# A macaron block (FFN, dilated attention, FFN) on one core: token mix taken from the PSUM tile, mask folded into the bias, square moved to ScalarE, projection operands split into 16-bit halves

## The chip, the cores and the metric

The kernel runs on one core of a Trainium2 chip. The core has a matrix engine (TensorE, PE in the profile; its weight loads have a row of their own, PEld), a vector engine (VectorE, DVE), a scalar engine (ScalarE, ACT), a general engine (GpSimd, POOL) and a queue engine (SyncE, SP) that issues most of the transfers. The engines run side by side, each takes its instructions in a fixed order, and they wait for one another through semaphores. Matrix products are written to PSUM, everything else lives in SBUF; the transfers go between SBUF and the device's memory.

The metric is the device time of one execution in microseconds (us). The time before is given as the median of three runs, and one further execution was recorded with the profiler.

## The reference, cut to what matters

There are 8 sequences of 1024 tokens with 256 channels, and 16 heads of 16 channels. Three residual steps follow one another: half an FFN, the attention, and half the same FFN.

```python
x = x + 0.5 * ffn(layernorm(x));  x = x + attn(layernorm(x));  x = x + 0.5 * ffn(layernorm(x))

def ffn(x):
    x_prev = shift x by one token (zero at the start of a sequence)
    xr = mu_r * x + (1 - mu_r) * x_prev
    xk = mu_k * x + (1 - mu_k) * x_prev
    return sigmoid(xr @ W_r) * (square(relu(xk @ W_k)) @ W_v)

def attn(x):
    q, k, v = split(x @ qkv_w.T + qkv_b)
    for i, o in enumerate(OFFSETS):            # 0..32, 48, 64, 96, 128, 192, 256, 384
        lg = (q . shift(k, o)) * inv * (1 + q . scale_embed[i]) + pos_bias[i]
        lg = where(pos >= o, lg, -1e30)
    p = softmax over the offsets
    out = (sum over i of p[i] * shift(v, o)) * if_gain
    return (out * sigmoid(x @ gate_w.T + gate_b)) @ out_w.T + out_b
```

## The kernel before, in words

The work is cut into 32 chunks of 256 tokens (two blocks of 128) and, for the attention proper, into 64 blocks of 128 tokens. Five stages are written as Python generators:

- `stage_f1`, the first FFN, one chunk a step, loads the chunk and leaves it in `x1`;
- `stage_p`, the projections of a chunk to q, k, gate and v, which sends q and k (as 16-bit high and low halves, tile `hl`) and v to device memory in layouts from which later stages read them back;
- `stage_qk`, the score products of half a sequence, copied out of PSUM by L308 and written to device memory, from which they are read back skewed, so that one offset is one column;
- `stage_att`, one block: the logits in tile `lg` (128 x 40 offsets x 16 heads), the softmax, the far offsets as products on POOL (L445) added up on DVE (L457), the near ones as matrix products (L464 transposes, then `pv`), the gate and the output projection;
- `stage_f2`, the second FFN, which also stores the result.

The order of the work is set in three ways. The last lines (L515 to L522) sort the steps of the five stages by hand-set offsets, `TRACE` for the order in which they are traced and `RANK` for their priority. The tile framework then fixes every engine's order of instructions at build time, from these priorities and a simulated timeline. On the chip each engine follows that order and stops at the first instruction whose inputs or buffers are not there. Every PSUM tag has one buffer: an FFN lane (`a` or `b`) has a single bank for its transposed input `tr` and then, one after the other, for the three products `p`, so each of them needs the one before to have been read.

One FFN chunk (`ffn`, L165 to L215) goes like this. `norm_stats` makes mean and 1/sd (DVE, and six small POOL instructions). `norm_transposed` applies them on ACT (L160) and transposes the chunk on PE (L162) into the PSUM tile `tr`, channels on partitions. ACT copies `tr` to the SBUF tile `xt` (L186), which is one column wider: POOL puts the last column of the previous chunk in front (L185, or L183 sets it to zero at the start of a sequence) and keeps the last column for the next one (L189). DVE takes the difference of the two shifted views (L193, 512 elements a partition) and then, twice for `xk` and twice for `xr`, adds mu times the difference to the shifted view (L196, 256 elements each). PE multiplies `xk` by W_k (the K product), ACT applies relu (L201), POOL squares in place (L207). PE multiplies `xr` by W_r (the R product), ACT applies tanh (L206), PE multiplies the square by W_v (the V product), DVE combines (L212), and POOL adds the result to the chunk (L213). Tiles `xt`, `xk` and `xr` have one buffer for each lane. There are 64 such chunks in the two stages.

In `stage_p` (L233 to L295) the transposed chunk is split into `xh` (F32R, copied on ACT, L244) and the rest `xl` (L245, DVE); `wa_hi` and `wa_lo` are the same split of the weights, made in `load_att`. Each of the four projections is 12 matrix products of 256 columns: high by high, high by low and low by high (L134 is the helper that issues every product). In `stage_att`, POOL adds the position bias to the logits (L419) and, for the first three of the eight blocks of a sequence, the mask (L421).

Of the kernel before, what the change touches and what calls it, by code (L numbers as in the profile page):

```python
# [8 lines left out]
F32 = mybir.dt.float32  # L9
F32R = mybir.dt.float32r  # L10
F16 = mybir.dt.float16
I32 = mybir.dt.int32
AF = mybir.ActivationFunctionType
ALU = mybir.AluOpType
# [25 lines left out]
F2A = 28  # L40
TRACE = (0, 3.6, -4.4, -8.1, -10.6)
# [8 lines left out]
def macaron(ctx: ExitStack, tc: tile.TileContext, x, wffn, watt, wo, cols, rows, pbias, se, mask, out):  # L50
# [14 lines left out]
    bias = const.tile([128, NO * 16], F32, name="bias")  # L65
    msk = const.tile([128, 3, NO], F32, name="msk")
    wa_hi = const.tile([128, 4, 2, 256], F32R, name="wa_hi")
    wa_lo = const.tile([128, 4, 2, 256], F32R, name="wa_lo")
    seb = const.tile([128, 2, NO], F16, name="seb")
    half = const.tile([128, 4], F32, name="half")  # L70
# [18 lines left out]
    def load_ffn():  # L89
        nc.sync.dma_start(w_f, wffn.rearrange("w (c p) d -> p w c d", p=128))  # L90
        nc.vector.tensor_scalar(w_f[:, 2], w_f[:, 2], 0.25, None, ALU.mult)

    def load_att():
        with tc.tile_pool(name="setup", bufs=1) as sp:
            wst = sp.tile([128, 4, 2, 256], F32, name="wst")
            nc.sync.dma_start(wst, watt.rearrange("w (c p) d -> p w c d", p=128))
            nc.vector.tensor_scalar(wst[:, 0], wst[:, 0], 0.25, None, ALU.mult)
            nc.vector.tensor_copy(wa_hi, wst)
            nc.vector.tensor_tensor(wa_lo, wst, wa_hi.bitcast(F32), ALU.subtract)
            nc.vector.tensor_scalar(b_q, b_q, 0.25, None, ALU.mult)  # L100
            nc.vector.tensor_scalar(b_g, b_g, 0.5, None, ALU.mult)
            nc.sync.dma_start(row, rows.unsqueeze(0).to_broadcast([128, 2, 256]))
            for t in [t.bitcast(F32) for t in kb] + vw:
                nc.gpsimd.memset(t, 0.0)
# [8 lines left out]
            nc.sync.dma_start(bias, pbias.to_broadcast([128, NO * 16]))  # L113
            nc.sync.dma_start(msk, mask.rearrange("t p u -> p t u"))
            nc.sync.dma_start(wot, wo.rearrange("(c p) d -> p c d", p=128))
            for c in range(2):
                nc.vector.tensor_scalar(wot[:, c], wot[:, c], gain[:, c : c + 1], 0.5, ALU.mult, ALU.mult)
# [47 lines left out]
    def ffn(take, done, lane, singles):  # L165
# [3 lines left out]
        for c in range(NCH):  # L169
# [11 lines left out]
            xt = pw.tile([128, 2, 257], F32, name="xt", tag="xt" + s)  # L181
            if c % 4 == 0:
                nc.gpsimd.memset(xt[:, :, 0:1], 0.0)  # L183
            else:
                nc.gpsimd.tensor_copy(xt[:, :, 0:1], last)  # L185
            nc.scalar.copy(xt[:, :, 1:257], tr)  # L186
            if c % 4 < 3:
                last = pstat.tile([128, 2, 1], F32, name="last", tag="last" + s)
                nc.gpsimd.tensor_copy(last, xt[:, :, 256:257])  # L189
            xk = pw.tile([128, 2, 256], F32, name="xk", tag="xk" + s)  # L190
            xr = pw.tile([128, 2, 256], F32, name="xr", tag="xr" + s)
            prev = xt[:, :, 0:256]
            nc.vector.tensor_tensor(xr, xt[:, :, 1:257], prev, ALU.subtract)  # L193
            for o, mu in ((xk, mu_k), (xr, mu_r)):
                for h in range(2):
                    nc.vector.scalar_tensor_tensor(o[:, h], xr[:, h], mu[:, h : h + 1], prev[:, h], ALU.mult, ALU.add)  # L196
# [10 lines left out]
            nc.gpsimd.tensor_tensor(xk, xk, xk, ALU.mult)  # L207
# [25 lines left out]
    def stage_p():  # L233
        for c in range(NCH):
# [7 lines left out]
            xh = pw.tile([128, 2, 256], F32R, name="xh", tag="xk" + s)  # L242
            xl = pw.tile([128, 2, 256], F32R, name="xl", tag="xr" + s)
            nc.scalar.copy(xh, tr)  # L244
            nc.vector.tensor_tensor(xl, tr, xh.bitcast(F32), ALU.subtract)  # L245
# [26 lines left out]
            for g in range(2):  # L272
                nc.scalar.activation(gt[:, g], p[:, g], AF.Tanh, bias=b_g[:, g : g + 1], scale=0.5)
# [312 lines left out]
```

## Time and profile before

| | |
|---|---|
| Median of 3 runs | 1262.62 us (1255.21 to 1265.52) |
| The profiled execution | 1256.76 us |
| Its span, from the first to the last instruction | 1254.0 us |
| Mean granted TensorE clock | 0.956 |
| Device-memory traffic over the span | 224 GB/s |
| Share of the span that the core's DMA engines were busy, slices of 50 us from 150 to 1150 us | 0.71 to 0.92 |
| PE busy in 50 us, over the same slices | 41.1 to 48.1 us |
| DVE busy in 50 us, over the same slices | 28.9 to 45.3 us |

The profile gives each engine's busy time and share, groups of instructions (line, engine, operation, output <- input, partitions x elements) with count, busy time and mean duration, the waits between engines, and the chain of work that ended last, followed back from the last instruction. A busy share of PE is not PE at its peak, since matrix products overlap and their ends are modelled. Between the profiled execution's time and its span lie 2.76 us.

### The profile page before, as it was taken

What the parts mean: (1) busy time and instruction counts of PE and PEld (TensorE: products, weight loads), DVE (VectorE), ACT (ScalarE), POOL (GpSimd) and SP (SyncE); (2) the same over time, 40 slices, a digit from 0 to 9 for tenths busy, and PEclk for the clock granted to TensorE, in tenths of its full rate; (3) what the DMA queues carried; (4) which work ended last, traced back from release to release, by engine and by line L of the source; (5) the groups of instructions that cost most, each with busy time, mean ns of one, the idle gap of its engine ahead of it and who ended that gap; (6) DMA issues with size and microseconds to landing.
All of it is one profiled execution on the core that took longest, in us unless ns stands there. A gap on an engine that the chain in (4) does not pass through costs nothing.

```text
span 1254.0 us, 34712 instructions
## 1 busy us (share of the span) xinstructions
PE 1089.2 (87%) x13568; PEld 885.7 (71%) x13568; DVE 942.6 (75%) x2266; ACT 538.0 (43%) x1025; POOL 766.5 (61%) x1101
## 2 busy tenths in 40 slices
PE   2887989899799898989899989899988998888785
PEld 2676768677687677777777778786777787665664
DVE  7546768987587888879678866978858887877772
ACT  2444445344453444536345454544534444524231
POOL 7436619675575656659457564867656755657672
PEclk9999999899999999899999999999989999998988
DMA  8187888786878779787788977797787868998630
GB/s 263 32 224 222 241 242 265 229 238 194 251 226 254 230 233 274 221 252 232 193 260 257 254 201 230 228 269 227 233 243 234 269 197 254 284 280 265 202 99 24
DMA packets 256500, 282.88 MB, mean 226 GB/s; under 512 B 23440, under 2 KB 214608, under 8 KB 256336
## 3 DMA queue, kind: packets, MB, share of 16 engines
q1 hardware_dynamic: 247120, 263.36, 71.7%
q10 hardware_dynamic: 9216, 17.31, 3.8%
q8 instruction: 106, 1.74, 0.6%
q14 instruction: 58, 0.48, 0.1%
HBM read 151.67 MB, written 128.91 MB: 224 GB/s over the span
## 4 chain that ended last, share of the span: by engine, by line
PE 42%; DMA 25%; DVE 14%; SPq 6%; POOL 5%; issue 5%; ACT 4%; POOLq 0%; ACTq 0%; DVEq 0%
PE p L134 29%; DMA pd<-pd 9%; PE tra L464 4%; PE pv L134 3%; PE tra L134 3%; POOL prod L445 2%; DMA lg<-sl 2%; DMA x<-in_x_dram 2%; DMA qk<-hl 2%; DMA kb<-qk 2%; DMA sl<-sl 2%; DVE prod L457 2%; DVE xk L196 1%; PE gp L134 1%; DVE mx L423 1%
## 5 line engine op out<-in xcount | busy, mean ns | idle before, releaser
L134 PEld LDWEIGHTS <-qst 128*32 128x32 f16 (+1 forms) x5120 | 157.2, 120 | 100.1 <-issue 63.5
L134 PE MATMUL p<-kb,qst 128*32 128x128 f16 (+1 forms) x4096 | 185.1, 297 | 12.7 <-ACT sl L308 8.6
L308 ACT COPY sl<-p 128x512 f32<-128x512 f32 x224 | 130.8, 584 | 144.2 <-PE p L134 123.0
L445 POOL TENSOR_TENSOR prod<-v,lg 128x256 f32<-128x256 f32 x248 | 165.5, 687 | 10.2 <-ACT lg L425 6.1
L134 PE MATMUL p<-xk,w_f 128*128 128x256 f32 x512 | 144.9, 421 | 20.0 <-DVE xk L196 11.7
L419 POOL TENSOR_TENSOR lg<-lg,bias 128x640 f32<-128x640 f32 x64 | 113.5, 1774 | 71.8 <-DVE lg L410 66.9
L213 POOL TENSOR_TENSOR x<-x,xr 128x512 f32<-128x512 f32 x64 | 88.4, 1382 | 109.0 <-DVE xr L212 94.9
L457 DVE TENSOR_TENSOR prod<-prod 128x512 f32<-128x512 f32 (+2 forms) x120 | 126.1, 1051 | 32.1 <-POOL prod L445 31.5
L464 PE MATMUL tra<-ident,pd 128*128 128x128 f32 x512 | 97.1, 313 | 58.3 <-DMA pd<-pd 54.9
L160 ACT ACTIVATE xn<-x,nb,y 128x256 f32<-128x256 f32 x192 | 110.8, 602 | 63.0 <-DVE nb L152 55.2
L134 PE MATMUL p<-w_f,xk 128*128 128x256 f32 x512 | 132.9, 400 | 1.7 <-ACT xr L206 1.3
L134 PE MATMUL p<-w_f,xr 128*128 128x256 f32 x512 | 130.4, 396 | 3.6 <-ACT xk L201 2.8
L445 POOL TENSOR_TENSOR prod<-vn,lg 128x256 f32<-128x256 f32 x144 | 96.0, 678 | 54.3 <-ACT lg L425 35.4
L134 PE MATMUL p<-xh,wa_hi 128*128 128x256 f32 x384 | 123.2, 321 | 5.6 <-DVE hl L264 4.4
L134 PEld LDWEIGHTS p<-xk,w_f 128*128 128x128 f32 x512 | 99.3, 208 | 39.8 <-issue 10.5
L470 ACT COPY ptt<-tra 128x512 f32<-128x512 f32 x128 | 74.9, 585 | 116.1 <-PE tra L464 113.0
L464 PEld LDWEIGHTS tra<-ident,pd 128*128 128x128 f32 x512 | 71.0, 197 | 73.9 <-DMA pd<-pd 68.0
L263 ACT ACTIVATE hl<-p,col 128x256 f16<-128x256 f32 x128 | 60.6, 474 | 121.1 <-PE p L134 68.6
L134 PE MATMUL p<-xh,wa_lo 128*128 128x256 f32 x384 | 111.5, 290 | 0.0
L134 PE MATMUL p<-xl,wa_hi 128*128 128x256 f32 x384 | 111.4, 290 | 0.0
L134 PEld LDWEIGHTS p<-w_f,xr 128*128 128x128 f32 x512 | 95.3, 196 | 19.4 <-ACT xk L201 5.8
L134 PEld LDWEIGHTS p<-w_f,xk 128*128 128x128 f32 x512 | 96.0, 198 | 15.9 <-issue 2.8
(82 smaller groups left out, 2394.2 us busy)
## 6 DMA issues: line engine op xcount, KB each, us to landing
qk<-hl SPq DMA_DIRECT2D x256, 128.0 KB, 3.4
sl<-sl SPq DMA_DIRECT2D x256, 128.0 KB, 3.8
pd<-pd SPq DMA_DIRECT2D x64, 512.0 KB, 4.8
sf<-sl SPq DMA_DIRECT2D x184, 128.0 KB, 3.1
vw<-vd SPq DMA_DIRECT2D x128, 136.0 KB, 4.1
v<-vd SPq DMA_DIRECT2D x64, 272.0 KB, 4.3
lg<-sl SPq DMA_DIRECT2D x64, 264.0 KB, 4.1
pd<-lg ACTq DMA_DIRECT2D x64, 264.0 KB, 3.8
```

What stands on the lines that cost most here:

```text
L134: nc.tensor.matmul(o, l, r, start=start, stop=stop)
L160: nc.scalar.activation(xn, x2[:, i], AF.Identity, bias=nb[:, k : k + 1], scale=y[:, k : k + 1])
L196: nc.vector.scalar_tensor_tensor(o[:, h], xr[:, h], mu[:, h : h + 1], prev[:, h], ALU.mult, ALU.add)
L213: nc.gpsimd.tensor_tensor(x2, x2, xr, ALU.add)
L263: nc.scalar.activation(hl[:, 0], p[:, g], AF.Identity, bias=bb[:, g : g + 1])
L308: nc.scalar.copy(o[:, :, :, g], p.rearrange("n (q h j) -> n j h q", q=4, h=2))
L419: nc.gpsimd.tensor_tensor(la, la, bias, ALU.add)
L423: nc.vector.tensor_reduce(mx, lg.rearrange("p u e -> p e u"), AX.X, ALU.max)
L445: nc.gpsimd.tensor_tensor(prod[:, k], shifted[k][1]()[:, :, 0:16], lf[:, k].unsqueeze(2).to_broadcast([128, 16, 16]), ALU.mult,)
L457: nc.vector.tensor_tensor(o, terms[:, 0:m], terms[:, n - m : n], ALU.add)
L464: nc.tensor.transpose(tr[:, pr * 128 : pr * 128 + 128], pd.rearrange("p (m e) -> p m e", e=8)[:, :, 4 * g + pr], ident,)
L470: nc.scalar.copy(ptt.rearrange("p q n -> p (q n)"), tr)
```

## The change

It has four parts.

**Token mix.** The copy to `xt` and the difference go. For each of `xk` and `xr` and each half of the channels, ACT reads the PSUM tile and scales it by mu (the main term), and DVE adds (1 - mu) times the PSUM tile, shifted by one column, for columns 1 to 255. Column 0 gets its share of the previous chunk by one small POOL addition of `last`, which DVE has made from the last PSUM column (a product by `rest` = 1 - mu for all four). Both results are in one tile `xm`, with one buffer for each lane.

**Mask.** The bias tile becomes four: three with the mask of the first three blocks already added (three POOL additions in the setup), and one without.

**Square.** It moves from POOL (L207) to ACT.

**Projection.** `xh`, `xl`, `wa_hi` and `wa_lo` become F16 instead of F32R. The weights are multiplied by `WS` = 16 before the split, and the factor is taken out again where q.k is copied out of PSUM, in the gate's scale, in the logits' constant and in the output weights. The 12 products of a projection stay 12. `xh` and `xl` get buffers of their own.

```diff
+WS = 16.0
-    bias = const.tile([128, NO * 16], F32, name="bias")
-    msk = const.tile([128, 3, NO], F32, name="msk")
-    wa_hi = const.tile([128, 4, 2, 256], F32R, name="wa_hi")
-    wa_lo = const.tile([128, 4, 2, 256], F32R, name="wa_lo")
+    bias = const.tile([128, 4, NO, 16], F32, name="bias")
+    wa_hi = const.tile([128, 4, 2, 256], F16, name="wa_hi")
+    wa_lo = const.tile([128, 4, 2, 256], F16, name="wa_lo")
+    rest = const.tile([128, 4], F32, name="rest")
...
+        nc.vector.tensor_scalar(rest, col[:, 0:4], -1.0, 1.0, ALU.mult, ALU.add)
...
-            nc.vector.tensor_scalar(wst[:, 0], wst[:, 0], 0.25, None, ALU.mult)
-            nc.vector.tensor_copy(wa_hi, wst)
-            nc.vector.tensor_tensor(wa_lo, wst, wa_hi.bitcast(F32), ALU.subtract)
-            nc.vector.tensor_scalar(b_q, b_q, 0.25, None, ALU.mult)
+            nc.vector.tensor_scalar(wst[:, 0], wst[:, 0], 0.25 * WS, None, ALU.mult)
+            nc.vector.tensor_scalar(wst[:, 1:4], wst[:, 1:4], WS, None, ALU.mult)
+            nc.scalar.copy(wa_hi, wst)
+            nc.vector.tensor_tensor(wa_lo, wst, wa_hi, ALU.subtract)
+            nc.vector.tensor_scalar(b_q, b_q, 0.25 * WS, None, ALU.mult)
+            nc.vector.tensor_scalar(b_k, b_k, WS, None, ALU.mult)
...
+            nc.vector.tensor_scalar(bv, bv, WS, None, ALU.mult)
...
+            msk = sp.tile([128, 3, NO], F32, name="msk")
+            nc.sync.dma_start(bias[:, 3].rearrange("p u e -> p (u e)"), pbias.to_broadcast([128, NO * 16]))
             nc.sync.dma_start(msk, mask.rearrange("t p u -> p t u"))
+            for t in range(3):
+                nc.gpsimd.tensor_tensor(
+                    bias[:, t], bias[:, 3], msk[:, t].unsqueeze(2).to_broadcast([128, NO, 16]), ALU.add
+                )
...
-            xt = pw.tile([128, 2, 257], F32, name="xt", tag="xt" + s)
-            if c % 4 == 0:
-                nc.gpsimd.memset(xt[:, :, 0:1], 0.0)
-            else:
-                nc.gpsimd.tensor_copy(xt[:, :, 0:1], last)
-            nc.scalar.copy(xt[:, :, 1:257], tr)
+            xm = pw.tile([128, 2, 2, 256], F32, name="xm", tag="xm" + s)
+            for o, mu in ((1, mu_k), (0, mu_r)):
+                for h in range(2):
+                    x_, m = xm[:, o, h], rest[:, 2 * o + h : 2 * o + h + 1]
+                    nc.scalar.activation(x_, tr[:, h], AF.Identity, scale=mu[:, h : h + 1])
+                    nc.vector.scalar_tensor_tensor(x_[:, 1:256], tr[:, h, 0:255], m, x_[:, 1:256], ALU.mult, ALU.add)
+            if c % 4:
+                nc.gpsimd.tensor_tensor(xm[:, :, :, 0:1], xm[:, :, :, 0:1], last, ALU.add)
             if c % 4 < 3:
-                last = pstat.tile([128, 2, 1], F32, name="last", tag="last" + s)
-                nc.gpsimd.tensor_copy(last, xt[:, :, 256:257])
-            xk = pw.tile([128, 2, 256], F32, name="xk", tag="xk" + s)
-            xr = pw.tile([128, 2, 256], F32, name="xr", tag="xr" + s)
-            prev = xt[:, :, 0:256]
-            nc.vector.tensor_tensor(xr, xt[:, :, 1:257], prev, ALU.subtract)
-            for o, mu in ((xk, mu_k), (xr, mu_r)):
-                for h in range(2):
-                    nc.vector.scalar_tensor_tensor(o[:, h], xr[:, h], mu[:, h : h + 1], prev[:, h], ALU.mult, ALU.add)
+                last = pstat.tile([128, 2, 2, 1], F32, name="last", tag="last" + s)
+                nc.vector.tensor_tensor(
+                    last,
+                    tr[:, :, 255:256].unsqueeze(1).to_broadcast([128, 2, 2, 1]),
+                    rest.rearrange("p (o h u) -> p o h u", o=2, u=1),
+                    ALU.mult,
+                )
+            xk, xr = xm[:, 1], xm[:, 0]
...
-            nc.gpsimd.tensor_tensor(xk, xk, xk, ALU.mult)
+            nc.scalar.activation(xk, xk, AF.Square)
...
-            xh = pw.tile([128, 2, 256], F32R, name="xh", tag="xk" + s)
-            xl = pw.tile([128, 2, 256], F32R, name="xl", tag="xr" + s)
+            xh = pw.tile([128, 2, 256], F16, name="xh", tag="xh" + s)
+            xl = pw.tile([128, 2, 256], F16, name="xl", tag="xl" + s)
             nc.scalar.copy(xh, tr)
-            nc.vector.tensor_tensor(xl, tr, xh.bitcast(F32), ALU.subtract)
+            nc.vector.tensor_tensor(xl, tr, xh, ALU.subtract)
...
-            nc.scalar.copy(o[:, :, :, g], p.rearrange("n (q h j) -> n j h q", q=4, h=2))
+            nc.scalar.mul(o[:, :, :, g], p.rearrange("n (q h j) -> n j h q", q=4, h=2), WS**-3)
...
-            nc.gpsimd.tensor_tensor(la, la, bias, ALU.add)
-            if t < 3:
-                nc.gpsimd.tensor_tensor(lg, lg, msk[:, t].unsqueeze(2).to_broadcast([128, NO, 16]), ALU.add)
+            nc.gpsimd.tensor_tensor(la, la, bias[:, min(t, 3)].rearrange("p u e -> p (u e)"), ALU.add)
```

More of the change, by code (lines that the diff above doesn't have):

```diff
@@ L9 @@
 F32 = mybir.dt.float32
-F32R = mybir.dt.float32r
 F16 = mybir.dt.float16
@@ L112, in load_att @@
             nc.sync.dma_start(flat(pd_d, NL * 16, (4 * SKEW, 128), (SKEW, 4), (1, SKEW - NL * 16)), zero[:, : 4 * 512])
-            nc.sync.dma_start(bias, pbias.to_broadcast([128, NO * 16]))
+            msk = sp.tile([128, 3, NO], F32, name="msk")
+            nc.sync.dma_start(bias[:, 3].rearrange("p u e -> p (u e)"), pbias.to_broadcast([128, NO * 16]))
             nc.sync.dma_start(msk, mask.rearrange("t p u -> p t u"))
+            for t in range(3):
+                nc.gpsimd.tensor_tensor(
+                    bias[:, t], bias[:, 3], msk[:, t].unsqueeze(2).to_broadcast([128, NO, 16]), ALU.add
+                )
             nc.sync.dma_start(wot, wo.rearrange("(c p) d -> p c d", p=128))
             for c in range(2):
-                nc.vector.tensor_scalar(wot[:, c], wot[:, c], gain[:, c : c + 1], 0.5, ALU.mult, ALU.mult)
+                nc.vector.tensor_scalar(wot[:, c], wot[:, c], gain[:, c : c + 1], 0.5 / WS, ALU.mult, ALU.mult)
             se_f = sp.tile([128, NO], F32, name="se_f")
@@ L272, in stage_p @@
             for g in range(2):
-                nc.scalar.activation(gt[:, g], p[:, g], AF.Tanh, bias=b_g[:, g : g + 1], scale=0.5)
+                nc.scalar.activation(gt[:, g], p[:, g], AF.Tanh, bias=b_g[:, g : g + 1], scale=0.5 / WS)
             p = ps.tile([128, 512], F32, name="p", tag="ps" + s)
@@ L405, in stage_att @@
                 nc.vector.scalar_tensor_tensor(
-                    lg[:, 0:NL, e], gp[:, 0:NL], 1.0, lg[:, 0:NL, e], ALU.add, ALU.mult
+                    lg[:, 0:NL, e], gp[:, 0:NL], WS, lg[:, 0:NL, e], ALU.add, ALU.mult
                 )
@@ L412, in stage_att @@
                         gp[:, NL + k0 : NL + k1],
-                        1.0,
+                        WS,
                         ef[:, w0 : w1 + 1 : (w1 - w0) // (k1 - k0 - 1), e],
```

## The prediction

> **What bounds the kernel now.** I read the page first: the busy shares, then the chain that ended last.
>
> ```profile
> PE 1089.2 (87%) x13568; PEld 885.7 (71%) x13568; DVE 942.6 (75%) x2266; ACT 538.0 (43%) x1025; POOL 766.5 (61%) x1101
> ...
> PE 42%; DMA 25%; DVE 14%; SPq 6%; POOL 5%; issue 5%; ACT 4%; POOLq 0%; ACTq 0%; DVEq 0%
> PE p L134 29%; DMA pd<-pd 9%; PE tra L464 4%; PE pv L134 3%; PE tra L134 3%; POOL prod L445 2%; DMA lg<-sl 2%; DMA x<-in_x_dram 2%; DMA qk<-hl 2%; DMA kb<-qk 2%; DMA sl<-sl 2%; DVE prod L457 2%; DVE xk L196 1%; PE gp L134 1%; DVE mx L423 1%
> ```
>
> No engine is full all the time, and the end is passed from one to another: PE holds 42% of the chain, transfers 25%, DVE 14%. A microsecond taken from an engine is worth only the share of it that lies on the chain. I got those shares by going through the chain in windows of 20 us and adding its pieces by line: DVE 182.5 us in all, of it 10.3 on L193, 21.2 on L196 for `xk` and 15.0 for `xr`; POOL 63.4 (4.6 on the square, L207); ACT 46.9 (4.9 on the copy to `xt`, L186).
>
> Second, the groups by line and shape, for the price of what goes and of what is like what comes (last column: idle time before):
>
> ```profile
> L196 DVE SCALAR_TENSOR_TENSOR xk<-xr,col,xt 128x256 f32<-128x256 f32 x128 | 83.2, 689 | 0.5
> L196 DVE SCALAR_TENSOR_TENSOR xr<-xr,col,xt 128x256 f32<-128x256 f32 x128 | 82.3, 668 | 0.0
> ...
> L207 POOL TENSOR_TENSOR xk<-xk 128x512 f32<-128x512 f32 x64 | 74.0, 1156 | 53.1 <-ACT xk L201 52.6
> ...
> L193 DVE TENSOR_TENSOR xr<-xt 128x512 f32<-128x512 f32 x64 | 51.8, 810 | 10.8 <-ACT xt L186 10.7
> ...
> L425 ACT ACTIVATE lg<-lg 128x640 f32<-128x640 f32 x64 | 47.4, 741 | 58.9 <-DVE lg L424 25.5 <-POOL t L148 9.8 <-issue 8.8
> ...
> L186 ACT COPY xt<-tr 128x512 f32<-128x512 f32 x64 | 37.5, 586 | 6.5 <-PE tr L162 5.5 <-POOL t L149 0.9
> ...
> L421 POOL TENSOR_TENSOR lg<-lg,msk 128x640 f32<-128x640 f32 x24 | 31.7, 1323 | 0.6
> ...
> L273 ACT ACTIVATE gt<-p,col 128x256 f32<-128x256 f32 x64 | 26.8, 470 | 42.9 <-PE p L134 42.8
> ...
> L491 DVE SCALAR_TENSOR_TENSOR yt<-gt,tra 128x256 f32<-128x256 f32 x64 | 26.3, 410 | 24.7 <-PE tra L490 24.7
> ```
>
> A group's mean hides its spread, so third the tile views (shortest/median/longest ns):
>
> ```profile
> L196 DVE SCALAR_TENSOR_TENSOR xk<-xr,col,xt x128: 441/478/1785, 20.6 to 1239.1; 128x256 f32<-128x256 f32 x128
> ...
> L212 DVE SCALAR_TENSOR_TENSOR xr<-xr,p x64: 652/679/690, 35.4 to 1248.9; 128x512 f32<-128x512 f32 x64
> ```
>
> L196 reads two SBUF tiles and is stretched up to four times, while L212, which reads one operand from PSUM, never is. In the order of time the long ones lie beside running POOL instructions.
>
> **The token mix on DVE.** It goes from 51.8 + 83.2 + 82.3 = 217.3 us to 4 x 64 = 256 instructions of 255 elements, one operand in PSUM, one in SBUF. The nearest row is L491 (same operation, 256 elements, PSUM and SBUF): 410 ns, so 105.0 us. `last` is a tiny DVE read of PSUM like L481 (164 ns), 48 of them: 7.9 us. Sum 112.9, saved 104.4 us. Here the Trainium skill speaks against the change: its page "VectorE: DVE Perf Modes" (the section on the TRN2 errata) gives fixed costs of 58 cycles from SBUF and 120 from PSUM at 0.96 GHz, and its "Rules for kernel authors" advise copying PSUM to SBUF first where many operations follow. An estimate from that page: (58 + 256)/0.96 = 327 ns from SBUF against (120 + 255)/0.96 = 391 ns from PSUM, so the four additions cost 256 x 64 ns = 16 us more, only the difference (L193; by the page (58 + 512)/0.96 = 594 ns, 38 us) is saved, and with `last` 14 us remain of the 104. The row has 685 on the mean for SBUF and 410 for PSUM. I take the row, since the stretching is what this kernel pays. On the chain: L193 and L196 hold 46.5 us; at the same share of their work the new ones hold 46.5 x 112.9/217.3 = 24.2, so **-22.3 us** (by the page -46.5 x 14/217.3 = -3).
>
> **The token mix on ACT.** Four scalings of 256 elements from PSUM replace a copy of 512: L273 is such an instruction (PSUM, 256, one per-partition operand), 470 ns. 256 x 470 = 120.3 us for 37.5, +82.8 us. The square on ACT has no row of its own shape (512 elements from SBUF): L425 (640 elements from SBUF) bounds it from above at 741, L201 (512 from PSUM, 595) from below; I take 640, 41.0 us. Here the skill's page "ScalarE: Activation LUTs" (Rules for kernel authors) objects: products belong on VectorE. By the nearest row for that (L193, two SBUF operands, 512) the square would cost DVE 810 ns x 64 = 52 us of an engine that is 75% busy; ACT is 43% busy, so I follow the profile. At DVE's share on the chain (182.5/942.6 = 19%) the page's way would add 10 us, at ACT's (46.9/538.0 = 8.7%) 3.6. ACT rises to 538.0 + 82.8 + 41.0 = 662 us, 53%. On the chain: 8.7% x 123.8 = **+10.8 us**.
>
> **POOL** loses the square (74.0), the masks (31.7) and the column copies (L183 1.6, L185 14.3, L189 20.9): 142.5. It gets 48 small additions like L149 (290 ns), 13.9: net -128.6 us. At POOL's share on the chain (63.4/766.5 = 8.3%): **-10.6 us**. The square in itself is hidden: the V product needs its PSUM bank back from the tanh (L206), which comes after the R product; PE waited for the square 0.3 us in all. Without that cover, ACT's 640 ns still replace POOL's 1156 and a mean 1.4 us in POOL's queue.
>
> **Projection in 16 bits.** The order of time on PE shows what an F32R product takes from start to start:
>
> ```profile
> 678.06 0.29 PE L134 MATMUL p<-xl,wa_hi 128*128 128x256 f32 x1
> ...
> 678.18 0.28 PE L134 MATMUL p<-xh,wa_lo 128*128 128x256 f32 x1
> ...
> 678.30 0.28 PE L134 MATMUL p<-xh,wa_hi 128*128 128x256 f32 x1
> ```
>
> 0.12 us for 256 columns, while plain f32 products of the same size (8 in 1.89 us, less a tail of 0.38) step by 0.216. F32R is already the fast kind; the 16-bit form can't win a second factor of two. Bounds: nothing (other lanes' work fills the steps) to 12 ns a product (the F32R step is 118; half of the f32 step is 108). 1536 x 11 ns = 17 us of PE, x 42% = **-7 us**. Weight loads shrink from 196 to about 105 ns (the f16 row of that size), which overlap anyway.
>
> **With one answer.** L308's scaling instead of copying, the constants and the bias index: nothing, same instruction, same shape. The setup grows by three POOL additions (1323 each, 4.0 us), a 2048-element ACT copy and short DVE scalings, while the chain there runs through transfers and the SP queue until 26 us, and the first projection starts at 53 us; bounds 0 to +5, I take 0. No transfer is added or moved past a queue; the bias and mask loads stay where they are on SP.
>
> **What waits anew.** First, ACT's first scaling needs `xm`, which the last addition of the previous chunk (L213, POOL) still reads; behind it on ACT stand the copies of `sl`, `ptt` and `hl`. In the trace, the copy to `xt` began before the latest L213 had ended in 9 of 64 chunks, by 5.8 us in all: hidden. Second, the K product gets behind a POOL addition (column 0) and, since it needs the bank of `tr`, behind all four scalings and additions, `xr` too. POOL was late at L213 by a mean 1.04 us (up to 5.3), so the hop costs 1.04 + 0.29 us in 48 of 64 chunks, 1.0 us on the mean. Today (means over the 64 chunks, from the order of time) `xk` is complete 5.32 us after the copy to `xt` starts, `xr` 7.64 us, for 0.59 + 217.3/64 = 3.98 us of work: stretched 1.92 times by what else is in DVE's queue. The new work in line is 4 ACT steps (470, then 370 each, as the L273 pair ends after 840), one addition and `last`: 2.15 us, times 1.92 = 4.1, with the hop 5.1 us. The K product is late by -0.2 us: 0.
>
> **Sum:** -22.3 + 10.8 - 10.6 - 7 = -29.1 us: 1256.76 becomes 1227.7 for the profiled execution. The median of the runs shown lies 5.9 us above that execution, so for the median 1262.6 - 29.1 = **1234 us** (1233.5).
>
> **The rivals.** A: *the added latency doesn't shrink.* If the mix still takes 7.64 us from the copy to its end (ACT and DVE waiting for each other eight times a chunk) and POOL's hop comes on top, the K product starts 7.64 + 1.0 - 5.32 = 3.3 us later, and PE, in order, holds the products of other lanes behind it; behind those wait the copies of `sl` and `ptt` and the SP transfers. For this speaks that PE already waits for `xk`:
>
> ```profile
> PE p L134 <- DVE xk L196: 11.7, 13, 2.4
> ...
> PEld p L134 <- DVE xk L196: 9.2, 14, 1.9
> ```
>
> (total, times, longest), against it that it is only 13 of 64 chunks. The saving is eaten from 29.1/(64 x 0.42) = 1.1 us of lateness a chunk on; at 2 us it is 54 - 29 = +25, **1287 us**. B: *hidden anyway.* PE and the DMA engines set the pace, another chain of the same length takes over: **1258 us**. For it: PE is busy 41 to 48 of every 50 us and the DMA engines 71 to 92%. Against: DVE is on the chain with 14%. C: *DVE is the pace in its full stretches* (up to 45 of 50 us busy) and its relief counts in half instead of a fifth: -104.4/2 - 10.6 - 7 + 10.8 = -59: **1204 us**.
>
> **How the numbers follow.** My forecast 0.45 (its own range 1215 to 1248), A 0.24, B 0.17, C 0.14. About 1% is what a measurement of this kernel can tell from no change: below 1250 is faster, above 1275 slower. Faster: 0.44 + 0.14 = 0.58. Same: B, 0.01 of the forecast and 0.02 of A: 0.20. Slower: 0.22. The range: below, C with the square and the masks counted in full, about 1180; above, A at its 2 us, 1287, with 5 us of setup: 1290.
>
> **What would show it.** L196's heirs at 400 to 430 ns without a spread; ACT near 660, POOL near 640, DVE near 840 us; projection products 0.11 us apart. Wrong would be: PE's waits for the small POOL addition or the last addition of the mix above 30 us in all (A), ACT waits for L213 above 10 us, DVE additions from PSUM above 600 ns, or a chain with more transfers and no less total (B).

## The result and the profile after

The changed kernel takes **1292.5 us** (median of 4 runs, 1289.8 to 1300.7) against 1263.1 us of the kernel before in the same comparison: ratio **1.026**, 95% interval 1.021 to 1.032. It is slower, where 1234 us was forecast and 1290 was the end of the range. The profiled span grows from 1254.0 to 1290.9 us.

First the page of the changed kernel: the busy time of each engine, and below the chain that ended last.

```profile
PE 1072.7 (83%) x13568; PEld 846.4 (66%) x13568; DVE 833.0 (65%) x2253; ACT 649.2 (50%) x1282; POOL 610.9 (47%) x952
...
PE 36%; DMA 29%; DVE 10%; SPq 8%; POOL 8%; issue 5%; ACT 3%; POOLq 0%; ACTq 0%; DVEq 0%
```

The busy times are what the prediction said: DVE 833 (forecast near 840), ACT 649 (660), POOL 611 (640), PE 16 us less. In spite of that the span is 37 us longer. PE, which was idle for 1254.0 - 1089.2 = 165 us, is now idle for 1290.9 - 1072.7 = 218 us. On the chain transfers and SP's queue rise to 37% of the span from 31%. So the engines are not busier; somebody comes later.

Who comes later is seen in the groups by line and shape (busy us, mean ns of one | idle time of the engine just before, and what ended it):

```profile
L197 DVE SCALAR_TENSOR_TENSOR xm<-tr,rest,xm 128x255 f32<-128x255 f32 x256 | 120.3, 472 | 55.3 <-ACT xm L196 55.0
L196 ACT ACTIVATE xm<-tr,col 128x256 f32<-128x256 f32 x256 | 120.1, 473 | 82.0 <-DVE xm L197 73.4 <-PE tr L172 6.2 <-DVE vn L296 1.6
```

and the tile view (shortest/median/longest ns):

```profile
L196 ACT ACTIVATE xm<-tr,col x256: 450/473/531, 25.2 to 1273.6; 128x256 f32<-128x256 f32 x128
L197 DVE SCALAR_TENSOR_TENSOR xm<-tr,rest,xm x256: 384/476/494, 25.7 to 1274.1; 128x255 f32<-128x255 f32 x128
L213 ACT ACTIVATE xm<-p x64: 588/597/636, 35.2 to 1278.6; 128x512 f32<-128x512 f32 x64
L219 ACT ACTIVATE xm<-xm x64: 611/631/650, 35.8 to 1279.2; 128x512 f32<-128x512 f32 x64
```

The single instructions hold no surprise: 472 ns for the addition without a spread (410 forecast), 473 for the scaling (470), 631 for the square (640). What is new is the last column of the groups: ACT's scalings wait 73.4 us for DVE's additions, and DVE's additions 55.0 us for ACT's scalings. One chunk in the order of time shows how. Start, duration, instruction; in brackets the idle time before it:

```profile
662.52 0.46 ACT L196 ACTIVATE xm<-tr,col 128x256 f32<-128x256 f32 x1
...
664.46 0.47 DVE L197 SCALAR_TENSOR_TENSOR xm<-tr,rest,xm 128x255 f32<-128x255 f32 x1
...
664.96 0.47 ACT L196 ACTIVATE xm<-tr,col 128x256 f32<-128x256 f32 x1 [0.64 <-DVE xm L197]
...
665.47 0.48 DVE L197 SCALAR_TENSOR_TENSOR xm<-tr,rest,xm 128x255 f32<-128x255 f32 x1 [0.16 <-ACT xm L196]
...
665.99 0.47 ACT L196 ACTIVATE xm<-tr,col 128x256 f32<-128x256 f32 x1 [0.55 <-DVE xm L197]
...
667.14 0.48 DVE L197 SCALAR_TENSOR_TENSOR xm<-tr,rest,xm 128x255 f32<-128x255 f32 x1
...
667.65 0.47 ACT L196 ACTIVATE xm<-tr,col 128x256 f32<-128x256 f32 x1 [1.19 <-DVE xm L197]
...
668.27 0.45 DVE L197 SCALAR_TENSOR_TENSOR xm<-tr,rest,xm 128x255 f32<-128x255 f32 x1
```

It is a **relay**: scaling, addition, scaling, addition; no scaling begins before the addition ahead of it has ended, although it doesn't use its result. Eight steps of 0.47 us would be 3.8 us; here it is 6.2, on the mean over the 64 chunks **9.71 us** (shortest 4.07), because at the hand-overs the next instruction stands in the queue of the other engine behind foreign work: 1.09 us on the mean from a scaling's end to its addition, 0.52 us from an addition's end to the next scaling. 4 x 1.09 + 3 x 0.52 + 3.8 = 9.7. (Two chunks are often in work at once; scalings and additions were put to their chunks by the tiles of the instruction lists.) Before, `xk` was complete 5.32 us after the copy began.

That this is so by construction can be read from the order that the framework built. For one chunk, each instruction with the engine whose semaphore it waits for (my summary of both instruction lists, not a profile):

```
changed kernel                    the same eight instructions, scalings first (experiment below)
ACT scaling  xk h0  waits PE      ACT scaling  xk h0  waits PE
DVE addition xk h0  waits ACT     ACT scaling  xk h1
ACT scaling  xk h1  waits DVE     ACT scaling  xr h0
DVE addition xk h1  waits ACT     ACT scaling  xr h1
ACT scaling  xr h0  waits DVE     DVE addition xk h0  waits ACT
DVE addition xr h0  waits ACT     DVE addition xk h1
ACT scaling  xr h1  waits DVE     DVE addition xr h0
DVE addition xr h1  waits ACT     DVE addition xr h1
```

The scalings share with the additions only the PSUM tile `tr`, which both read, and different parts of `xm`. What waits longer after that, the list of waits tells (total us, times, longest). Before:

```profile
POOL x L213 <- DVE xr L212: 94.9, 29, 9.5
...
DVE hl L264 <- ACT hl L263: 24.4, 27, 3.7
...
PE gp L134 <- DVE lg L410: 10.1, 9, 2.4
...
PE p L134 <- DMA kb<-qk: 1.6, 1, 1.6
```

After:

```profile
POOL x L225 <- DVE xm L224: 186.9, 40, 15.2
...
ACT xm L196 <- DVE xm L197: 73.4, 68, 6.6
...
DVE xm L197 <- ACT xm L196: 55.0, 60, 4.8
...
DVE hl L276 <- ACT hl L275: 43.8, 47, 3.4
...
PE gp L144 <- DVE lg L422: 22.8, 16, 6.6
...
PE p L144 <- DMA kb<-qk: 20.5, 8, 7.7
```

The end of the chunk (POOL's addition into `x`) waits twice as long for the product before it, the split of q and k (`hl`) is later, and the score products wait 20.5 instead of 1.6 us for `kb`, which is read back from the `qk` that `hl` was written to. This reads as if the lateness of an FFN chunk went on through `x1`, the projection, `qk` and the readback to PE; that path is not shown (it stays open below).

What these lists do not have is a long wait of PE for the mix itself:

```profile
PE p L144 <- DVE xm L197: 4.8, 2, 4.2
...
PE p L144 <- POOL xm L199: 0.2, 1, 0.2
...
PEld p L144 <- POOL xm L199: 13.1, 6, 6.3
```

Before, PE waited 11.7 us for `xk` and its weight loads 9.2. The delay is in PE's fixed order instead. Counted in the instruction lists, 73.5 of PE's products stand between a chunk's last transpose and its K product before (mean of 64 chunks), and 122.3 in the changed kernel: the build, which orders PE by a simulated timeline, has placed the K product behind 49 more products of other work. So a late chunk is measured from its transposes to its relu, and not by a wait for it.

### The profile page after: what moved, and what is told of

Its sections match the earlier page's. It is cut to its first block, busy times and chain, and to the rows that moved or that the text cites. A ratio compares the mean times of both kernels' runs of the same rounds, so it can differ in the third digit from the quotient of the medians.

```text
span 1290.9 us, 34761 instructions
## 1 busy us (share of the span) xinstructions
PE 1072.7 (83%) x13568; PEld 846.4 (66%) x13568; DVE 833.0 (65%) x2253; ACT 649.2 (50%) x1282; POOL 610.9 (47%) x952
## 4 chain that ended last, share of the span: by engine, by line
PE 36%; DMA 29%; DVE 10%; SPq 8%; POOL 8%; issue 5%; ACT 3%; POOLq 0%; ACTq 0%; DVEq 0%
PE p L144 24%; DMA pd<-pd 9%; DMA qk<-hl 4%; PE tra L474 4%; POOL prod L455 4%; DMA sl<-sl 3%; DMA lg<-sl 3%; PE pv L144 2%; DMA x<-in_x_dram 2%; SPq L374 2%; DMA kb<-qk 2%; PE tra L144 2%; DMA pd<-lg 2%; DVE xm L197 2%; SPq L331 2%
## 5 line engine op out<-in xcount | busy, mean ns | idle before, releaser
L144 PE MATMUL p<-w_f,xm 128*128 128x256 f32 x1024 | 257.4, 396 | 7.2 <-ACT xm L218 6.2
L144 PE MATMUL p<-kb,qst 128*32 128x128 f16 (+1 forms) x4096 | 187.9, 298 | 41.4 <-DMA kb<-qk 20.5
L144 PEld LDWEIGHTS p<-w_f,xm 128*128 128x128 f32 x1024 | 190.9, 196 | 37.3 <-ACT xm L218 7.7
L320 ACT ACTIVATE sl<-p 128x512 f32<-128x512 f32 x224 | 133.4, 596 | 124.1 <-PE p L144 92.9
L196 ACT ACTIVATE xm<-tr,col 128x256 f32<-128x256 f32 x256 | 120.1, 473 | 82.0 <-DVE xm L197 73.4
L144 PE MATMUL p<-xm,w_f 128*128 128x256 f32 x512 | 141.5, 423 | 22.2 <-DVE mv L153 6.7
L197 DVE SCALAR_TENSOR_TENSOR xm<-tr,rest,xm 128x255 f32<-128x255 f32 x256 | 120.3, 472 | 55.3 <-ACT xm L196 55.0
L144 PEld LDWEIGHTS p<-xm,w_f 128*128 128x128 f32 x512 | 103.3, 213 | 42.0 <-POOL xm L199 13.1
L144 PE MATMUL p<-xh,wa_hi 128*128 128x256 f16 x384 | 106.2, 277 | 6.3 <-DVE hl L276 4.7
L144 PEld LDWEIGHTS pv<-vw,ptt 128*32 128x32 f32 x4096 | 87.6, 154 | 30.3 <-issue 17.1
L144 PE MATMUL p<-xh,wa_lo 128*128 128x256 f16 x384 | 105.8, 276 | 0.0
```

The lines of the kernel that those rows point to most:

```text
L144: nc.tensor.matmul(o, l, r, start=start, stop=stop)
L196: nc.scalar.activation(x_, tr[:, h], AF.Identity, scale=mu[:, h : h + 1])
L197: nc.vector.scalar_tensor_tensor(x_[:, 1:256], tr[:, h, 0:255], m, x_[:, 1:256], ALU.mult, ALU.add)
L320: nc.scalar.mul(o[:, :, :, g], p.rearrange("n (q h j) -> n j h q", q=4, h=2), WS**-3)
```

## The experiments

Theory **R** (relay): the new mix takes longer from the transposes to the K product, because ACT and DVE hand the work to and fro; the late chunk costs the time (this second half is called **L**, lateness, in the later expectations), the engines' load doesn't. Rivals: **Q** (load: ACT's 111 us more are on the path), **H** (POOL's hop on column 0), **T** (the start: the first work begins late), **S** (ACT's and DVE's queues stand still while the two wait for each other, and a late chunk is covered), **O** (something other than the mix). Each ratio is against the kernel before on the same chip, with its 95% interval. Two measures of a chunk come from the order of time, as means over 64 chunks: from the end of its transposes to the start of the relu, and to the end of the combination (L212 before, L224 after).

### Which part loses

**The new mix alone on the kernel before**, with everything else as it was:

```diff
-            nc.scalar.copy(xt[:, :, 1:257], tr)
...
-            nc.vector.tensor_tensor(xr, xt[:, :, 1:257], prev, ALU.subtract)
-            for o, mu in ((xk, mu_k), (xr, mu_r)):
...
+            for o, mu in ((1, mu_k), (0, mu_r)):
...
+                    nc.scalar.activation(x_, tr[:, h], AF.Identity, scale=mu[:, h : h + 1])
+                    nc.vector.scalar_tensor_tensor(x_[:, 1:256], tr[:, h, 0:255], m, x_[:, 1:256], ALU.mult, ALU.add)
```

> The kernel before with the new token mix alone. Theory R: it bears the whole loss and lacks the small gains of the rest, 1295 to 1310 us, with the mix near 9.7 us from the first scaling to the last addition. Rival Q: less than the full change, since the square is not on ACT, 1270 to 1285 us. Rival O: no slower than the kernel before, 1235 to 1265 us.

Measured: 1320.4 us, **1.048** [1.040, 1.055]; mix 9.02 us, relu after 16.27 us (before 10.40). The loss is larger than every range given for it.

**All the rest without the mix** (square, mask, 16-bit halves; the old mix put back):

```diff
-                    nc.scalar.activation(x_, tr[:, h], AF.Identity, scale=mu[:, h : h + 1])
-                    nc.vector.scalar_tensor_tensor(x_[:, 1:256], tr[:, h, 0:255], m, x_[:, 1:256], ALU.mult, ALU.add)
...
+            nc.scalar.copy(xt[:, :, 1:257], tr)
...
+            nc.vector.tensor_tensor(xr, xt[:, :, 1:257], prev, ALU.subtract)
```

> The changed kernel with the old token mix put back (copy to xt, difference, four L196 additions): square, mask and 16-bit projection remain. Theory R (relay: the new mix passes the PSUM tile from ACT to DVE and back eight times, and that is what costs): these three parts alone gain 5 to 15 us on the kernel before, about 1251 us. Rival Q (ACT has too much work, the square included): 1262 to 1275 us. Rival O (one of the other three parts, or the new order that they cause, is what costs): above 1280 us.

Measured: 1266.9 us, 1.007 [1.004, 1.009]. The gain that R expected is missing, and the time lies in Q's range; Q is put to the test next. The mix alone loses and the rest alone hardly does, so O falls as the main cause. The two don't add up (4.8% and 0.7% against 2.6% together).

### Why the mix loses

**The same eight instructions, four scalings first, then four additions** (one hand-over instead of seven), all else of the change kept:

```diff
                 for h in range(2):
+                    nc.scalar.activation(xm[:, o, h], tr[:, h], AF.Identity, scale=mu[:, h : h + 1])
+            for o in (1, 0):
+                for h in range(2):
                     x_, m = xm[:, o, h], rest[:, 2 * o + h : 2 * o + h + 1]
-                    nc.scalar.activation(x_, tr[:, h], AF.Identity, scale=mu[:, h : h + 1])
```

> The changed kernel with the eight instructions of the mix in another order: all four scalings on ACT, then all four additions on DVE; same work, one hand-over instead of seven. Theory R: the mix shrinks from 9.7 us to about 5.5 us (2.15 us of work in a row and one wait in each queue), and the time falls to 1235 to 1265 us. Rival Q: ACT has the same work, so the time stays at 1285 to 1295 us.

Measured: 1256.9 us, **0.996** [0.994, 0.998], some 35 us below the changed kernel. In its order of time the relay is gone; one line now holds all four instructions:

```profile
694.23 1.58 ACT L195 ACTIVATE xm<-tr,col 128x256 f32<-128x256 f32 x4
...
695.91 1.65 DVE L199 SCALAR_TENSOR_TENSOR xm<-tr,rest,xm 128x255 f32<-128x255 f32 x4 [0.53 <-POOL prod L457]
```

The mix takes 4.85 us instead of 9.71, the relu starts 11.01 us after the transposes instead of 15.50. The page has the same work on every engine:

```profile
PE 1069.7 (85%) x13568; PEld 842.5 (67%) x13568; DVE 821.8 (66%) x2253; ACT 637.2 (51%) x1282; POOL 616.4 (49%) x952
```

This is the experiment that decides: the same instructions on the same engines (ACT 637 us busy, still 99 more than before), and 35 us less time. PE is busy equally long in both (1069.7 and 1072.7 us), so what is gone is idle time of PE; 76.9 products now stand between transposes and K product instead of 122.3. Q falls as the cause of this loss. It does not follow that ACT's load costs nothing (below).

**Two scalings, two additions, twice** (three hand-overs), a point between:

```diff
+                    nc.scalar.activation(xm[:, o, h], tr[:, h], AF.Identity, scale=mu[:, h : h + 1])
+                for h in range(2):
                     x_, m = xm[:, o, h], rest[:, 2 * o + h : 2 * o + h + 1]
-                    nc.scalar.activation(x_, tr[:, h], AF.Identity, scale=mu[:, h : h + 1])
```

> The changed kernel with the mix in pairs: two scalings, two additions for xk, then the same for xr; three hand-overs between ACT and DVE where the changed kernel has seven and the reordered one has one. Theory R: the cost goes with the hand-overs, so a third of the way from one to seven: mix near 6.5 us, time near 1269 us (1262 to 1276). If a single return from DVE to ACT were enough to lose all: 1285 us or more.

Measured: 1274.9 us, 1.013 [1.007, 1.020]; mix 6.95 us, relu at 13.69 us. As R expected. With seven, three and one hand-over: 9.71, 6.95, 4.85 us of mix, 122, 99, 77 products ahead of the K product, 1292, 1275, 1257 us of time.

**Without the hop**: the changed kernel without `last` and without POOL's addition to column 0.

```diff
-            if c % 4:
-                nc.gpsimd.tensor_tensor(xm[:, :, :, 0:1], xm[:, :, :, 0:1], last, ALU.add)
-            if c % 4 < 3:
-                last = pstat.tile([128, 2, 2, 1], F32, name="last", tag="last" + s)
...
```

> The changed kernel without last and without the POOL addition to column 0: it leaves out what the last token of the previous chunk gives to the first of this one. It tells what the POOL hop ahead of the K product costs. Theory R: little, 1280 to 1292 us, since POOL waits for ACT alone and was done 0.3 us before the last addition on the mean. Rival H (the hop is the cause): 1240 to 1270 us.

Measured: 1285.8 us, 1.018 [1.012, 1.025]; relu at 15.36 us (15.50 with the hop). In the changed kernel the hop ends 0.32 us *before* the last addition on the mean, and after it in 13 of 48 chunks: mostly hidden. H is at most some 0.8% (1.026 to 1.018, intervals that overlap), not the cause.

**Lateness without a relay**: the kernel before, with `xr` mixed ahead of `xk`. The same work on the same engines, only the K product's input comes later.

```diff
-            nc.vector.tensor_tensor(xr, xt[:, :, 1:257], prev, ALU.subtract)
-            for o, mu in ((xk, mu_k), (xr, mu_r)):
+            nc.vector.tensor_tensor(xk, xt[:, :, 1:257], prev, ALU.subtract)
+            for o, mu in ((xr, mu_r), (xk, mu_k)):
```

> The kernel before with xr mixed ahead of xk: the same instructions on the same engines, no relay, no PSUM tile shared, but xk, which the K product needs, is complete about 2.3 us later in each chunk. Theory L (what the relay costs is lateness of the K product): the change made relu start 5.1 us later in a chunk and the reordered mix 0.6 us later, for 35 us between the two, about 8 us for each us, so 2.3 us cost 18 us: 1275 to 1285 us. Rival S (what costs is that ACT's and DVE's queues stand still at their heads while the two wait for each other; a late K product is covered by other lanes): 1255 to 1266 us.

Measured: 1294.8 us, **1.028** [1.022, 1.033]; the relu starts 12.43 us after the transposes, 2.03 later than before. Its waits look like those of the changed kernel:

```profile
PE p L134 <- DMA kb<-qk: 20.9, 8, 5.0
...
PE p L134 <- DVE xk L196: 19.7, 14, 3.8
```

PE itself waits only 8 us more for `xk` than the 11.7 of before, but again 20 us for `kb`. So a late K product costs time without any relay, which is the second half of R, and S falls. The size is above the expected range: twice as much for each us of lateness as in the relay (worked out below). What else this order changes was not taken apart.

### What the parts are worth

**The reordered mix alone on the kernel before** (square on POOL): is a mix without relay a gain?

```diff
+                    nc.scalar.activation(xm[:, o, h], tr[:, h], AF.Identity, scale=mu[:, h : h + 1])
+            for o in (1, 0):
+                for h in range(2):
...
```

> The kernel before with the new token mix alone, in the order with one hand-over (four scalings, then four additions), square on POOL. The full change in that order took 0.4% less than the kernel before, the square alone 1.6% less. If the relay was all that was wrong with the mix, the mix alone is worth what was forecast for it: 1235 to 1250 us. If the mix is worth nothing even without the relay, and the square is what helps: 1262 to 1285 us.

Measured: 1268.5 us, 1.005 [1.003, 1.008]. No: 95 us less of DVE buy nothing. Against the first experiment the relay's price is 1.048/1.005, 4.2%.

**The square alone on ACT**:

```diff
-            nc.gpsimd.tensor_tensor(xk, xk, xk, ALU.mult)
+            nc.scalar.activation(xk, xk, AF.Square)
```

> The kernel before with the square alone moved to ACT. It is hidden behind the R product: 1250 to 1270 us. If POOL's queue held up the chain: below 1250 us. If ACT's load costs: above 1270 us.

Measured: 1247.3 us, **0.984** [0.978, 0.989]. The square ends 0.98 us after the relu instead of 2.52. That is the range for "POOL's queue held up the chain".

```profile
PE 1091.2 (87%) x13568; PEld 889.8 (71%) x13568; DVE 918.8 (74%) x2266; ACT 577.5 (46%) x1089; POOL 695.7 (56%) x1037
```

**Is that only another order of instructions?** The framework's order hangs on hand-set priorities; one of them moved by 0.1 shows how much a mere reordering does. Without and with the square on ACT:

```diff
-RANK = (0, 5.1, -4.4, -8.1, -10.6)
+RANK = (0, 5.0, -4.4, -8.1, -10.6)
```

> The kernel before with one constant of the hand-set order changed (RANK of the second FFN from 5.1 to 5.0): the same instructions in another order on every engine. It tells how far the time moves by the order alone. Theory L holds as it stands if the time stays at 1250 to 1272 us; if it moves by 20 us or more, single differences of that size (the 8 us of the three other parts, the 23 us between the two placements of the mask) are no evidence for a cause.

> The square on ACT together with the changed constant of the order (RANK 5.0 instead of 5.1), which alone made 0.35% more. If the gain of the square comes from what it does to POOL's queue, it stays in another order: 1.2% or more less than that kernel, 1240 to 1258 us. If it was a lucky order: 1262 to 1275 us.

Measured: 1.0035 [1.001, 1.006] without, 0.990 [0.987, 0.993] with the square: 0.990/1.0035 is again 1.3% for the square. So the gain isn't one lucky order. One reordering alone made 0.35%, so a single difference of that size says nothing.

**The 16-bit projection alone**, and **with the mask merged into the bias** (`msk` loaded and added in `stage_att`, ahead of the first three blocks, as here):

```diff
-    wa_hi = const.tile([128, 4, 2, 256], F32R, name="wa_hi")
+    wa_hi = const.tile([128, 4, 2, 256], F16, name="wa_hi")
...
-            xh = pw.tile([128, 2, 256], F32R, name="xh", tag="xk" + s)
+            xh = pw.tile([128, 2, 256], F16, name="xh", tag="xh" + s)
...
```

> The kernel before with the 16-bit projection alone. 1536 products at 0.11 instead of 0.12 us on an engine that holds some 40% of the chain: 7 us less, 1248 to 1260 us. Order alone could move it by more.

> The 16-bit projection and the mask folded into the bias ahead of the first three logits, square on POOL, old token mix. The same as the 1243.5 us kernel without the square on ACT: if the gain of that kernel comes from the two, 1240 to 1250 us; if from the square, 1255 to 1262 us.

Measured: 0.998 [0.995, 1.001] and 0.998 [0.996, 1.001]. Neither does anything that can be measured, though PE is busy for 1070.6 instead of 1089.2 us.

### The start

In the changed kernel three POOL additions stand ahead of the first `y` of the normalisation, and wait for the mask's transfer:

```profile
12.77 3.84 POOL L122 TENSOR_TENSOR bias<-bias,msk 128x640 f32<-128x640 f32 x3 [0.82 <-DMA msk<-in_mask_dram]
16.57 2.85 POOL L157 TENSOR_TENSOR y<-va,half 128x2 f32<-128x2 f32 x1
...
22.86 1.18 PE L172 MATMUL tr<-ident,xn 128*128 128x128 f32 x4 [22.86 <-ACT xn L170]
```

Before, that `y` began at 11.13:

```profile
11.13 1.50 POOL L147 TENSOR_TENSOR y<-va,half 128x2 f32<-128x2 f32 x1
...
17.60 1.18 PE L162 MATMUL tr<-ident,xn 128*128 128x128 f32 x4 [17.60 <-ACT xn L160]
```

The first transposes come 5.3 us later. Two kernels move the mask's transfer and the additions out of the setup, one on the reordered mix, one on the kernel with the old mix and all the rest:

```diff
-            nc.sync.dma_start(msk, mask.rearrange("t p u -> p t u"))
-            for t in range(3):
...
+            if tt < 3:
+                if tt == 0:
+                    nc.sync.dma_start(msk, mask.rearrange("t p u -> p t u"))
+                nc.gpsimd.tensor_tensor(
...
```

> The changed kernel with the eight instructions reordered (scalings first), and the mask folded into the bias one block at a time ahead of the first three logits instead of in the setup, so that the three POOL additions no longer stand ahead of the first chunk's 1/sd. If the start sets the end, the 5 us by which the first transposes are late come back: 1257 - 5, about 1252 us (1248 to 1255). If the late start is absorbed: 1255 to 1260 us.

> The changed kernel with the old token mix, and with the mask folded in ahead of the first three logits instead of in the setup. If the late start is what made mask, square and 16 bits together 8 us slower than the kernel before: 1258 to 1262 us. If not: 1264 to 1270 us, and the cause lies in one of these parts or in the order of the work.

Measured: 1266.6 us, 1.003 [1.001, 1.005], and **1243.5 us, 0.985** [0.980, 0.991]. The first transposes start earlier in both (19.83 for 22.70, 18.60 for 23.32). Yet the first is 0.7% slower than without the move, the second 2.1% faster than its own, both outside the ranges expected for them. T is not settled: the 5.3 us are real, but the move has opposite signs in the two kernels, and what else it reorders was not separated.

### A mix that can't relay

**The kernel with the square on ACT; the copy to `xt` is kept, ACT scales from `tr`, DVE adds from `xt`**, so that the two engines no longer read the same PSUM tile:

```diff
-            nc.vector.tensor_tensor(xr, xt[:, :, 1:257], prev, ALU.subtract)
...
+                    nc.scalar.activation(o[:, h], tr[:, h], AF.Identity, scale=mu[:, h : h + 1])
+                    nc.vector.scalar_tensor_tensor(o[:, h], prev[:, h], m, o[:, h], ALU.mult, ALU.add)
```

> The square on ACT, and a mix that keeps the copy to xt and its column 0, drops the difference, scales on ACT from PSUM and adds on DVE from xt in SBUF: ACT and DVE share no PSUM tile, so no scaling waits for DVE. Theory L (the latency of an FFN chunk sets the time, about 11 us of time for 1 us of it): one DVE step less ahead of xk, 0.5 us or more earlier, 5 us less than the square alone: 1238 to 1247 us. If ACT's load counts (120 us more, 700 us in all): above 1255 us.

Measured: 1261.9 us, 0.999 [0.997, 1.002]: a miss. Two things come out of it. In its groups no scaling waits for an addition, though they are written in turn, as in the changed kernel:

```profile
L199 DVE SCALAR_TENSOR_TENSOR xk<-xt,rest,xk 128x256 f32<-128x256 f32 x128 | 86.4, 700 | 20.4 <-ACT xk L198 20.4
L199 DVE SCALAR_TENSOR_TENSOR xr<-xt,rest,xr 128x256 f32<-128x256 f32 x128 | 75.5, 616 | 0.0
...
L198 ACT ACTIVATE xr<-tr,col 128x256 f32<-128x256 f32 x128 | 55.6, 501 | 0.0
L198 ACT ACTIVATE xk<-tr,col 128x256 f32<-128x256 f32 x128 | 54.9, 489 | 0.0
```

Both halves of `xk` still lie in one tile here, written by both engines. This points to the shared PSUM tile as what the framework serializes; two PSUM tiles with one reader each were not tried. And its chunk is the quickest of all (relu after 8.07 us, combination after 21.72, against 10.43 and 23.84 with the square alone), but the 1.6% of the square are gone. A quicker chunk is no gain by itself, where a slower one is a loss.

The time lies where the expectation put a cost of ACT's load (above 1255 us). Three comparisons have the scalings on ACT without a relay, and all three lose against the old mix: alone (1.005), here against the square alone (0.999/0.984, 1.6%), and with the mask at its blocks (1.003/0.985, 1.8%). ACT is busy for 59 to 86 us more in them. Whether that load is the cause was not tested.

## Why the prediction was wrong, point by point

- **The failed step** is in "What waits anew": "The new work in line is 4 ACT steps (470, then 370 each, as the L273 pair ends after 840), one addition and `last`: 2.15 us, times 1.92 = 4.1, with the hop 5.1 us. The K product is late by -0.2 us: 0." It takes the four scalings as back to back, with one hand-over to DVE. The built order has seven, and each takes a place in a queue: 9.71 us. The relu starts 5.1 us later instead of 0.2 us earlier. Where the instructions really follow one another so (scalings first), the estimate of 4.1 us (5.1 with the hop) is near: 4.85. The sentence "ACT and DVE waiting for each other eight times a chunk" stood in rival A at 0.24; A is what happened, with a mix even longer than its 7.64 us, though the sign set for A, PE's waits for the hop or the last addition above 30 us, stayed away (5.0 us on PE, 13.1 on its weight loads): the lateness went into PE's order. What could have been seen beforehand is that scaling and addition alternate in the source; that the framework makes the next scaling wait for the addition could not be seen in the trace of before, where DVE never reads `tr` in the FFN, and should have been bounded from both sides: 4.1 us without, 8 x 0.47 x 1.92 = 7.2 us with the waits.
- **The price of lateness** in A (64 x 0.42 = 27 us of time for each us per chunk) was too high. Against the scalings-first kernel the changed one lost 37.8 us of span for 4.49 us (8 per us), the pairs 19.0 for 2.68 (7), and `xr` first lost 38.4 against the kernel before for 2.03 (19). So A's 1287 us came out near the 1292 by luck, from a lateness taken too small and a price taken too high. The price is no constant either, as the 19 shows.
- **The end of the range**: "1287, with 5 us of setup" is 1292 and not 1290. The lower end doesn't follow from its terms either: with the square and the masks in full (105.7 us, of which C has 8.8), C's 1204 would be about 1107 and not 1180.
- **DVE's -22.3 us on the chain**: the busy time fell as forecast (943 to 833 us), the time didn't: the reordered mix alone is 0.5% slower. There DVE's part of the chain is 160.4 us, against 179.4 before (added over the whole chain; the windows of the prediction gave 182.5), so some 19 us did leave it, and PE's part grew from 524 to 558 us and that of the transfers from 309 to 321. That is rival B's argument, right for this part: other work took the place. The share of an engine on the chain is no price for its work.
- **Row or page**: the row was the better guide to the old mix, because its means hold a stretching that the page's fixed costs don't have. The fixed costs of the Trainium skill's "VectorE: DVE Perf Modes" (the section on the TRN2 errata) give, as an estimate, 391 ns for an addition from PSUM and 327 from SBUF. Measured, one addition from PSUM lasts 472 ns, but four in a row take 1.65 us, so the next starts after (1.65 - 0.47)/3 = 0.39 us: the page's estimate fits this step, the row's 410 is 62 ns short of the duration. From SBUF the median duration is the same (478 and 476 ns); the means of 689 and 668 (678 together, not 685) come from additions that are stretched. In the trace of the kernel before, the 90 of 256 beside which POOL was idle took at most 485 ns, and POOL was busy for 61% or more of each of the 85 that took over 600.
- **ACT +10.8 us**: not the loss of the change, since scalings-first has the same load at 0.996. But scalings-first is 1.3% slower than the square alone, as are the other mixes with scalings on ACT (above), so this term may well be real; it is not shown.
- **POOL -10.6 us, the square "in itself hidden"**: wrong in the good direction. Alone it gives 1.6%, about 20 us of the 1267.9 measured beside it (1.3% in the other order). In the kernel before the square ended after the tanh in 6 of 64 chunks, 9.2 us in all, and never on ACT; the rest is not pinned down (POOL has 71 us less to do, and the chunk is 0.8 us shorter).
- **PE -7 us**: PE's busy time fell by 18.6 us (17 forecast), the time by nothing (0.998). Between products 0.11 us as forecast:

```profile
500.31 0.27 PE L144 MATMUL p<-wa_hi,xl 128*128 128x256 f16 x1
500.42 0.27 PE L144 MATMUL p<-wa_hi,xh 128*128 128x256 f16 x1
500.53 0.27 PE L144 MATMUL p<-wa_lo,xh 128*128 128x256 f16 x1
```

- **Setup, bounds 0 to +5, taken 0**: the first transposes are 5.3 us late. The additions took 1.28 us each as priced (1.32); overlooked was where they stand, ahead of the first normalisation in POOL's order, and that they wait for a transfer there.
- **The hop, 1.0 us**: mostly hidden, since column 0 needs only the scalings (0.32 us ahead of the last addition).

Both kernels are beaten by the square alone (1247.3 us, 0.984) and by the old mix with the square, the halves and the mask added at its blocks (1243.5 us, 0.985); their intervals overlap. **Open** stays why a mix with less DVE work and a quick chunk gives nothing (ACT's load is untested), what moving the mask out of the setup is worth by itself, and by which path the square gains. The way from a late chunk to PE (`x1`, projection, `qk`, `kb`) is read from the waits of two kernels, not shown by taking it away. Scalings-first waits 11.5 us for `kb` without a loss, and the pairs 27.4 us with half the loss, so the `kb` wait is a sign at most and not the measure.

## What to carry to other kernels

Price a split of work between two engines by its hand-overs too, and not by its busy time alone: count them in the built order, give each the mean time of the other engine's queue, and try all the instructions of the first engine ahead of those of the second. When the chain changes hands among engines and transfers, ask first what becomes later for the next product, and look for it in the built order: a framework that foresees the delay places other work ahead, and no wait shows it. Less work on one engine may be worth nothing (95 us of DVE) or much (71 us of POOL); an experiment with that part alone tells. And measure what a mere reordering does (here 0.35%; moving a transfer and three additions came with +0.7% in one kernel and -2.1% in another) before a small difference is given a cause.

## What the runs showed of the hardware

- DVE's three-operand addition of 255 elements takes 472 ns with one operand in PSUM, at most 494 in 256 instances; of 256 elements with both in SBUF 616 to 700 on the mean, with a median of 476 to 478, and in the kernel before up to 1785 beside POOL, never over 485 with POOL idle.
- Four scalings from PSUM back to back take 1.58 us on ACT, so 0.37 us each after the first; alone, each takes 0.47. Four additions on DVE take 1.65. A relay loses this overlap as well: 120 us of busy time for 100 (ACT) and 106 (DVE).
- Of the same square, 512 elements from SBUF, ACT makes 631 ns and POOL 1156.
- The projection's 16-bit weights load in 99 ns instead of 196, which brought no time here (0.998).
- The granted TensorE clock was 0.956 before, 0.938 after and 0.927 for the mix alone (profiled executions), while PE was idle for 165, 218 and 206 us: the lowest clock doesn't go with the most idle time. The 16-bit projection alone had 0.939 on the mean of its runs, the kernel before beside it 0.948, at the same time (0.998). What brings a lower clock, and what it costs, these runs don't separate.
